# Ternary signs prepared in the offset stage, and the hats of tile columns loaded from ScalarE's queue

## Chip, cores, metric

One core of one Trainium2 chip. The metric is the time on the device of one execution, in microseconds (us). The four executions of the kernel before agree within 0.2% (7741.9 to 7756.0 us), those of the changed kernel within 0.5% (8181.8 to 8218.1). All executions that were timed in rounds ran in the fast state; runs of one look have no state of their own; the kernel before, run beside them, took 7741 to 7753 us (medians). The engines are PE (TensorE), DVE (VectorE), ACT (ScalarE), POOL (GpSimd) and SP (SyncE, which here only issues transfers, 5,333 in the kernel before).

## The reference, cut to what matters

```python
def _branch(x, w_off, w_def, lw, lb, pad, dil):          # dil = pad = 1, 9, 12
    off = _conv(x, w_off, pad, dil)                      # offsets, 18 channels
    y = _deform_dw(x, off, w_def, pad, dil)              # bilinear samples, 9 taps
    return gelu(_ln2d(y, lw, lb))
...
out = _ln2d(x1 + x2 + x3 + conv1x1(x), n1_w, n1_b)       # then an MLP and another _ln2d
...
def _L1_conv_ref(x, weight, bias, Wp, Wn):
    wq = _quantize(weight, Wp, Wn)                       # +Wp, 0 or -Wn by a threshold on max|w|
    return conv3x3(x, wq) + bias
...
x = x + _L0_conv_ref(_gn(x), ...)                        # x: (2, 256, 128, 128) float32
x = x + _L1_conv_ref(_gn(x), ...)
```

## The kernel before

It has three stages. The **offset stage** normalises `x`, computes the offsets of all branches and writes "hats" (the weights of bilinear interpolation along rows and along columns) to memory. The **sampling stage** treats 402 units: 2 batches x 67 tile rows x 3 branches. A unit loads three row hats `hy` and three column hats `hx`, DVE multiplies them to `A`, PE samples by multiplying the table's tiles `xs` with `A`, ACT copies each product to `ev`, DVE adds `ev` into `ring`. A tail (norms, MLP) is woven in. The **convolution stage** works with signs of the weights.

```python
def load_tiles(b, Rt):
    for T in range(NT):                                            # 14 tiles
        xt = pool.tile([P, C], F32, name="xs", tag="xs", bufs=20)
        ...
        nc.sync.dma_start(xt, src)

def load_hats(u):
    for ky in taps(u):                                             # up to three
        hy = pool.tile([P, RI, 3, W], F32, name="hy", tag="hy", bufs=3)
        hx = pool.tile([P, RI, 3, W], F32, name="hx", tag="hx", bufs=3)
        for h, first, dims in ((hy, ...), (hx, ...)):
            nc.sync.dma_start(h[...], ...)                         # both from SyncE

def sample(u, c):                                                  # two passes, c = 0 and 1
    ev = pool.tile([P, 9 * RI, NT * CI], F32, name="ev", tag="ev", bufs=2)
    for T in range(0, NT, 2):
        if T // 2 == NT // 4:
            tail.advance()
        pm = psum.tile([P, 2, 256], F32, name="pm", tag="pm", bufs=4)
        for j in range(2):
            pin(nc.tensor.matmul(pm[:, j, 0:n], lhsT=xts[...], rhs=A[...], ...))
        pin(nc.scalar.copy(ev[...], pm[...]))
    if c == KC - 1:
        prepare(u + 2)                     # build(u + 2), then load_hats(u + 3)
    accumulate(u, c, ev, kys)
...
# offset stage: statistics of each batch, through three buffers
xt = ap.tile([P, XT * NG], F32, name="xt", tag="xt", bufs=3)
nc.sync.dma_start(xt, ...)
nc.vector.bn_stats(...)
...
# convolution stage
signs = cp.tile([P, KC, 9, C], BF16, name="signs")
quantise(cp, signs)                        # loads the weights, threshold, 18 x 3 instructions
```

`pin` keeps an instruction at its place in its engine's order.

Of the kernel before, what the change touches and what calls it, by code (L numbers as in the profile page):

```python
# [67 lines left out]
def conv_preact_kernel(ctx: ExitStack, tc: tile.TileContext, t: dict, out: bass.AP):  # L68
# [19 lines left out]

    def load(name, shape, src):
        tl = const.tile(shape, F32, name=name)  # L90
        nc.sync.dma_start(tl, src)
        return tl

    gmask = load("gmask", [P, P], t["gmask"])
    convs = [
# [18 lines left out]

    def dram(name, shape):
        return [scratch.tile(shape, F32, name=f"{name}{b}", tag=f"{name}{b}") for b in range(NB)]
# [8 lines left out]
    yd = scratch.tile([3, C, HW], F32, name="yd")  # L125

# [33 lines left out]
    def phase_a(b, pool, psum, k):  # L160
# [160 lines left out]
        for g in range(NGRP):  # L321
            columns(g)
            while G < H // ZG and min(H - 1, G * ZG + ZG - 1 + max(DILS)) < (g + 1) * R:
                parts = offsets(G)
                for j in range(ZG // R):
                    make_hats(G * (ZG // R) + j, parts, j * R)
                G += 1

    with ExitStack() as actx:
# [18 lines left out]
        nc.sync.dma_start(k["wz"], t["wz"].rearrange("(k p) n -> p k n", p=P))  # L348
        nc.sync.dma_start(k["shift"], t["shift"])
        hatw = ap.tile([P, 2, NTAP * NH], F32, name="hatw32")  # L350
        nc.sync.dma_start(hatw, t["hatw"])
        nc.vector.tensor_copy(k["hatw"], hatw)
        pattern = ap.tile([P, NG], F32, name="pattern")
        nc.sync.dma_start(pattern[HALF : HALF + NPAT], t["pattern"])
        for pl in k["planes"]:
            nc.vector.tensor_copy(
                pl[HALF : HALF + NPAT, 1, :], pattern[HALF : HALF + NPAT]
            )
        for parts in k["parts"]:
            nc.vector.memset(parts, 0.0)  # L360
        XT = min(4, NGRP)
        for b in range(NB):
            stats = ap.tile([P, KC, NGRP, 6], F32, name=f"stats1_{b}", tag=f"stats1_{b}")
            for c in range(KC):
                for g0 in range(0, NGRP, XT):
# [7 lines left out]
                    for j in range(XT):  # L373
                        nc.vector.bn_stats(stats[:, c, g0 + j, :], xt[:, j * NG : (j + 1) * NG])
            mean, rstd = group_norm(stats, f"gn1_{b}", gps)
# [7 lines left out]
            phase_a(b, ap, psum, k)  # L383
# [8 lines left out]
    beyond = nc.values_load(flag[0:1, 0:1], min_val=0, max_val=1)  # L392

# [231 lines left out]
    def sample_near(pool, psum, k):  # L625
# [4 lines left out]
        xts, hbs, owners, begun = {}, {}, {}, set()  # L630
        done = {(b, br): 0 for b in range(NB) for br in BRS}
# [23 lines left out]
        def load_hats(u):  # L655
            b, Rt, br = units[u]
            for ky in taps(u):
# [6 lines left out]
                for h, first, dims in (  # L664
                    (hy, 0, [[0, TC], [pitch, TR]]),
                    (hx, TR, [[pitch, TC], [0, TR]]),
                ):
                    src = hq[first, y0]
                    nc.sync.dma_start(
                        h[:, i0:i1].rearrange("p i t w -> p (i t w)"),  # L670
                        bass.AP(src.tensor, src.offset, dims + [[1, (i1 - i0) * 3 * W]]),
                    )
                hbs[u, ky] = hy, hx

# [67 lines left out]
        def sample(u, c):  # L742
# [4 lines left out]
            if not kys:  # L747
                tail.advance()
# [7 lines left out]
            for T in range(0, NT, 2):  # L756
                if T // 2 == NT // 4:
                    tail.advance()
                pm = psum.tile([P, 2, 256], F32, name="pm", tag="pm", bufs=4)
# [31 lines left out]
        load_hats(0)  # L791
        prepare(0)
        prepare(1)
        for u, (b, Rt, br) in enumerate(units):
# [128 lines left out]
    def quantise(pool, signs=None):  # L923

        wq = pool.tile([P, KC, 9, C], F32, name="wq", tag="wq", bufs=1)
        nc.sync.dma_start(wq, t["l1w"].rearrange("(k p) t o -> p k t o", p=P))
        scale = []
        for name in ("wp", "wn"):
            s = pool.tile([P, 1], F32, name=name, tag=name, bufs=1)
            nc.sync.dma_start(s, t[name].partition_broadcast(P))  # L930
            scale.append(s)
        wp, wn = scale
        nc.vector.tensor_scalar(wn, wn, -1.0, None, ALU.mult)

        def col(name):
            return pool.tile([P, 1], F32, name=name, tag=name, bufs=1)

        own, m, mh, ml, pr, er, z, nc_ = (
            col(f"q_{i}") for i in ("own", "m", "mh", "ml", "pr", "er", "z", "nc")
        )  # L940
        nc.vector.tensor_reduce(
            own, wq.rearrange("p k t o -> p (k t o)"), AX.X, ALU.max, apply_absolute_value=True
        )
        nc.gpsimd.partition_all_reduce(m, own, P, bass.bass_isa.ReduceOp.max)  # L944



        def ts(dst, a, s1, op0, s2=None, op1=None):
            nc.vector.tensor_scalar(dst, a, s1, s2, op0, *(() if op1 is None else (op1,)))

        ts(mh, m, 4097.0, ALU.mult)
        nc.vector.tensor_tensor(ml, mh, m, ALU.subtract)
        nc.vector.tensor_tensor(mh, mh, ml, ALU.subtract)
        nc.vector.tensor_tensor(ml, m, mh, ALU.subtract)
        ts(pr, m, THR, ALU.mult)
        nc.vector.scalar_tensor_tensor(er, mh, THR_HI, pr, ALU.mult, ALU.subtract)
        nc.vector.scalar_tensor_tensor(er, mh, THR_LO, er, ALU.mult, ALU.add)
        nc.vector.scalar_tensor_tensor(er, ml, THR_HI, er, ALU.mult, ALU.add)
        nc.vector.scalar_tensor_tensor(er, ml, THR_LO, er, ALU.mult, ALU.add)
        nc.vector.scalar_tensor_tensor(er, m, THR_HALF_ULP, er, ALU.mult, ALU.add)  # L960

        ts(z, m, 0.0, ALU.is_equal)
        nc.vector.tensor_tensor(pr, pr, z, ALU.add)
        ts(nc_, er, -1.0, ALU.mult)
        for k in range(KC):
            for tap in range(9):
                w = wq[:, k, tap, :]
                up = pool.tile([P, C], F32, name="up", tag="up", bufs=1)
                ts(up, w, pr, ALU.subtract, er, ALU.is_ge)
                dn = pool.tile([P, C], F32, name="dn", tag="dn", bufs=1)  # L970
                ts(dn, w, pr, ALU.add, nc_, ALU.is_le)
                if signs is not None:
                    nc.vector.tensor_tensor(signs[:, k, tap, :], up, dn, ALU.subtract)  # L973
                    continue
                ts(up, up, wp, ALU.mult)
                nc.vector.scalar_tensor_tensor(w, dn, wn, up, ALU.mult, ALU.add)
        return wq

# [51 lines left out]
    def phase_c_signs(b, pool, psum, cring, signs, sums, wp, half):  # L1030
# [9 lines left out]
        JC = RC // 2  # L1040
        for g in range(H // RC):
# [4 lines left out]
            for k in range(KC):  # L1046
                nc.sync.dma_start(xl[:, k, rows, :], xv[:, k, lo:hi, :])
            xc = cring[g % len(cring)]
            for k in range(KC):
# [16 lines left out]
                left = D.rearrange("p i j w -> p (i j) w")  # L1066
                for i in range(2):
                    part = xc[:, i, k, :, 1 : 1 + W]
                    nc.scalar.copy(part, left)  # L1069
                    nc.vector.tensor_tensor(  # L1070
                        left if i == 0 else xc[:, 2, k, :, 1 : 1 + W], left, part, ALU.subtract
                    )
            for m in range(KC):
                pc = psum.tile([P, 4, 512], F32, name="pc", tag="pc", bufs=2)

                for bank, t in ((0, 0), (1, 3), (2, 1), (3, 2)):
# [3 lines left out]
                    for j, (k, kx, i) in enumerate(todo):  # L1080
                        w = (
                            signs[:, k, (t // 3 * 2) * 3 + kx] if t % 3 == 0
                            else sums[:, k, t - 1, kx]
# [30 lines left out]

    wpn = small.tile([P, 2], F32, name="wpn", tag="wpn", bufs=1)
    for i, name in enumerate(("wp", "wn")):
        nc.sync.dma_start(wpn[:, i : i + 1], t[name].partition_broadcast(P))
    eq = const.tile([P, 1], I32, name="eq")
    nc.vector.tensor_tensor(eq, wpn[:, 0:1], wpn[:, 1:2], ALU.is_equal)
    same = nc.values_load(eq[0:1, 0:1], min_val=0, max_val=1)  # L1120

    with tc.If(same > 0) as cmp:  # L1122
        with ExitStack() as cctx:
# [10 lines left out]
            signs = cp.tile([P, KC, 9, C], BF16, name="signs")  # L1134
            quantise(cp, signs)

            sums = cp.tile([P, KC, 2, 3, C], BF16, name="sums")
            for k in range(KC):
                nc.vector.tensor_tensor(
                    sums[:, k, 0], signs[:, k, 0:3], signs[:, k, 6:9], ALU.add  # L1140
                )
                nc.vector.tensor_tensor(
                    sums[:, k, 1], sums[:, k, 0], signs[:, k, 3:6], ALU.subtract
                )
                nc.vector.tensor_tensor(
                    sums[:, k, 0], sums[:, k, 0], signs[:, k, 3:6], ALU.add
                )
            half = cp.tile([P, 2], F32, name="half")
            for i in range(2):
                nc.vector.tensor_scalar(  # L1150
                    half[:, i : i + 1], wpn[:, 0:1], 0.5 - i, None, ALU.mult
                )
            for b in range(NB):
                phase_c_signs(b, cp, psum, cring, signs, sums, wpn[:, 0:1], half)
# [102 lines left out]
```

## Time and profile before

| | before |
|---|---|
| median of all its runs beside the changed kernel | 7751.5 us |
| offset stage, first `pz` product to first `pm` product | 880 us |
| sampling stage, first `pm` to the last store of `x1d` | 5,696 us |
| convolution stage, from there to the end | 1,094 us |

From the page of the kernel before: the busy time of the engines, then groups of instructions (line, engine, operation, output<-inputs, count | busy, mean ns of one | idle time before them and what ended it).

```profile
PE 7065.1 (91%) x37984; PEld 5377.1 (69%) x37984; DVE 6136.4 (79%) x12892; ACT 4818.2 (62%) x10138; POOL 708.7 (9%) x1292
...
L762 PE MATMUL pm<-A,xs 128*128 128x180 f32 (+2 forms) x22288 | 3609.6, 318 | 466.8 <-ACT ev L771 438.3
```

PE is the fullest engine, and nearly all its idle time in the sampling stage is ended by ACT having copied a product. The 62% of ACT look like plenty of room. That this number misleads is one lesson of this case.

### The profile page before, as it was taken

To read this page: it belongs to the slowest core of one execution; us is meant where nothing else is said; L and a number is where in the kernel's file an instruction comes from. 1 tells how busy PE (TensorE), PEld (TensorE's weight loads), DVE (VectorE), ACT (ScalarE), POOL (GpSimd) and SP (SyncE) were. 2 spreads that over 40 slices of the span, in tenths; PEclk is the share of its full clock that TensorE was granted. 3 is DMA by queue.
4 is the path that set the end of the run, shared out by engine and by line. 5 is a ranking of instruction groups with operands and counts; after the bars stand their busy time and mean duration, and the time that the engine had idled before them with its cause. 6 is when DMAs were issued, how large, how long until landed. Compare 5 with 4: busy or idle time off the path is not lost. (4 is left out here: it accounts for less than half of the span.)

```text
span 7751.0 us, 115301 instructions
## 1 busy us (share of the span) xinstructions
PE 7065.1 (91%) x37984; PEld 5377.1 (69%) x37984; DVE 6136.4 (79%) x12892; ACT 4818.2 (62%) x10138; POOL 708.7 (9%) x1292
## 2 busy tenths in 40 slices
PE   5999888999999999999988999999999998699999
PEld 3555587787877788777777778777887776244444
DVE  6666568888888888888678888888888885677676
ACT  1344366777777777777766777777777776333232
POOL 0000000111111111111101111111111111000000
PEclk9999889999999999999999999999999998799999
DMA  8776799999999999998699999999999994212121
GB/s 296 212 197 190 191 235 249 249 255 251 246 252 252 252 247 251 254 245 229 184 235 247 255 249 250 247 251 255 247 249 253 251 241 133 85 74 75 70 75 49
DMA packets 1011325, 1652.64 MB, mean 213 GB/s; under 512 B 120800, under 2 KB 573200, under 8 KB 1006360
## 3 DMA queue, kind: packets, MB, share of 16 engines
q1 hardware_dynamic: 993304, 1611.57, 77.7%
q10 hardware_dynamic: 17408, 33.56, 1.4%
q8 instruction: 304, 4.98, 0.3%
q14 instruction: 309, 2.53, 0.1%
HBM read 1376.69 MB, written 268.09 MB: 212 GB/s over the span
## 5 line engine op out<-in xcount | busy, mean ns | idle before, releaser
L762 PE MATMUL pm<-A,xs 128*128 128x180 f32 (+2 forms) x22288 | 3609.6, 318 | 466.8 <-ACT ev L771 438.3
L762 PEld LDWEIGHTS pm<-A,xs 128*128 128x128 f32 x22288 | 3407.1, 195 | 680.7 <-ACT ev L771 545.8
L740 DVE SCALAR_TENSOR_TENSOR ring<-ev,defw,ring 128x256 f32<-128x256 f32 (+3 forms) x6272 | 2774.5, 462 | 359.7 <-ACT ev L771 175.2
L771 ACT COPY ev<-pm 128x360 f32<-128x360 f32 (+2 forms) x5572 | 2235.8, 455 | 1131.6 <-DVE ring L740 462.9
L689 DVE TENSOR_TENSOR A<-hy,hx 128x768 f32<-128x768 f32 x1130 | 1022.3, 946 | 424.2 <-DMA hx<-hats 246.5
L487 ACT ACTIVATE T<-T,rs 128x256 f32<-128x256 f32 x1280 | 662.5, 593 | 3.3 <-POOL rs L483 3.2
L480 POOL TENSOR_SCALAR rs<-mv 128x4 f32<-128x4 f32 x320 | 120.7, 377 | 4981.0 <-DVE mv L478 2392.1
L1085 PE MATMUL pc<-cring,signs 128*128 128x512 bf16 x2304 | 521.9, 385 | 57.8 <-DVE signs L973 24.3
L1085 PE MATMUL pc<-cring,sums 128*128 128x512 bf16 x2304 | 510.3, 380 | 0.0
L446 PE MATMUL hp<-T,w 128*128 128x512 f32 x1024 | 492.7, 606 | 12.9 <-ACT T L565 12.9
L476 DVE BATCH_NORM_STATS2 st<-T 128x6 f32<-128x256 f32 x1280 | 446.8, 411 | 23.6 <-ACT T L468 23.6
L1085 PEld LDWEIGHTS <-signs 128*128 128x128 bf16 x2304 | 227.3, 99 | 341.8 <-issue 46.6
L203 PE MATMUL pz<-wz,xa 128*128 128x486 f32 x1024 | 456.7, 579 | 4.3 <-DVE zr L210 4.3
L446 PE MATMUL h<-hT,w 128*128 128x512 f32 x1024 | 460.1, 592 | 0.0
L1085 PEld LDWEIGHTS <-sums 128*128 128x128 bf16 x2304 | 225.4, 98 | 274.4
L515 ACT ACTIVATE T<-zc,bb,bw 128x512 f32<-128x512 f32 x384 | 278.7, 781 | 220.2 <-PE zc L499 219.7
L733 ACT ACTIVATE ring<-ev,defw 128x256 f32<-128x256 f32 (+1 forms) x788 | 392.2, 503 | 24.1
L499 PEld LDWEIGHTS zc<-ident,T 128*128 128x128 f32 x2560 | 325.9, 151 | 97.5 <-issue 61.5
L1093 ACT ACTIVATE o<-xl,l1b 128x1024 f32<-128x1024 f32 x64 | 73.5, 1149 | 505.7 <-DMA out_x<-o 408.3
L499 PE MATMUL zc<-ident,T 128*128 128x128 f32 x2560 | 368.7, 289 | 20.1 <-ACT T L487 13.9
L1069 ACT CAST cring<-D 128x2048 bf16<-128x2048 f32 x128 | 243.3, 1902 | 225.0 <-PE pc L1085 153.7
L482 POOL TENSOR_TENSOR rs<-rs,mhalf 128x4 f32<-128x4 f32 x320 | 368.3, 1151 | 0.0
(120 smaller groups left out, 5814.0 us busy)
## 6 DMA issues: line engine op xcount, KB each, us to landing
hy<-hats SPq DMA_DIRECT2D x1114, 384.0 KB, 6.5
hx<-hats SPq DMA_DIRECT2D x1114, 384.0 KB, 7.4
xs<-table SPq DMA_DIRECT2D x1876, 128.0 KB, 4.4
g12d<-T SPq DMA_DIRECT2D x128, 512.0 KB, 7.5
other<-g12d SPq DMA_DIRECT2D x128, 512.0 KB, 10.3
hats<-hb SPq DMA_DIRECT2D x192, 240.0 KB, 4.3
hats<-hb SPq DMA_DIRECT2D x192, 192.0 KB, 3.4
xl<-x1d SPq DMA_DIRECT2D x56, 640.0 KB, 3.9
```

Of the source, the lines that this page charges most:

```text
L203: nc.tensor.matmul(pz[:, 0:NZ], lhsT=xt[:, c, r, :], rhs=k["wz"][:, c, :], start=c == 0, stop=c == KC - 1,)
L446: nc.tensor.matmul(out, lhsT=w, rhs=v, start=i == 0, stop=i == n - 1)
L476: pin(nc.vector.bn_stats(st[:, j, :], Tv[:, j, :]))
L482: nc.gpsimd.tensor_tensor(rs[:, 0, :], rs[:, 0, :], mhalf[:, 0:NB4], ALU.pow)
L487: nc.scalar.activation(Tv[:, j, :], Tv[:, j, :], AF.Identity, scale=rs[:, 0, j : j + 1], bias=rs[:, 1, j : j + 1],)
L499: nc.tensor.transpose(zc[:, j * P : (j + 1) * P], Tv[:, j, c * P : (c + 1) * P], ident)
L689: nc.vector.tensor_tensor(dst, hy[:, i0:i1].rearrange("p i t w -> p t i w"), hx[:, i0:i1].rearrange("p i t w -> p t i w"), ALU.mult,)
L733: pin(nc.scalar.mul(dst, src, w))
L740: pin(nc.vector.scalar_tensor_tensor(dst, src, w, dst, ALU.mult, ALU.add))
L762: nc.tensor.matmul(pm[:, j, 0:n], lhsT=xts[b, Rt][T + j][:, c * P : (c + 1) * P], rhs=A[:, m0:m1, AO + (T + j) * CI : AO + (T + j + 1) * C ...
L771: nc.scalar.copy(ev[:, m0:m1, T * CI : (T + 2) * CI].rearrange("p m (t j) -> p t m j", j=CI), pm[:, :, 0:n].rearrange("p t (m j) -> p t m ...
L1085: nc.tensor.matmul(pc[:, bank, :], lhsT=w[:, m * P : (m + 1) * P], rhs=xc[:, i, k, t * JC : (t + 1) * JC, kx : kx + W], start=j == 0, stop ...
```

## The change

Three things were meant: let `x` go ahead of the constants at the start; take the signs out of the convolution's start by working them out amid the offset stage, where PE is the limit (busy 177.9 of 180 us); and let column hats no longer stand in SyncE's order behind tiles that wait for buffers. The core of the diff (cut; the loads of constants, and a finer split of the first convolution group, are left out):

```diff
+    def store_signs(pool):                       # a generator, one step per column group
+        w = pool.tile([P, 5, C], F32, name="wk", tag="xt", bufs=3)   # shares xt's buffers
+        ...
+            nc.sync.dma_start(signd[:, k], sg)
@@ offset stage
             columns(g)
+            next(beside, None)
@@ load_hats
-                    nc.sync.dma_start(
+                    args = (
                         h[:, i0:i1].rearrange("p i t w -> p (i t w)"),
                         bass.AP(src.tensor, src.offset, dims + [[1, (i1 - i0) * 3 * W]]),
                     )
+                    if h is hy:
+                        nc.sync.dma_start(*args)
+                    else:
+                        asked.append(args)
+        def load_columns():
+            while asked:
+                pin(nc.scalar.dma_start(*asked.popleft()))
@@ sample
                 if T // 2 == NT // 4:
                     tail.advance()
+                    load_columns()
@@ convolution stage
-            signs = cp.tile([P, KC, 9, C], BF16, name="signs")
-            quantise(cp, signs)
+            signs = cp.tile([P, KC, 15, C], BF16, name="signs")
...
+            if first:
+                nc.sync.dma_start(signs, signd)
```

## The prediction

> **What bounds the kernel now.** The program runs in three stages: offsets, deformable sampling with a tail of norms and MLP woven in, then the ternary convolution. I read the windows view first, with edges where the line groups change.
>
> ```profile
> core 0: us, PE busy (x) PEld busy (x) DVE busy (x) ACT busy (x) POOL busy (x), PEclk, DMA share, GB/s
> 250.00:430.00 180.00, 177.90 (x741) 100.41 (x741) 115.91 (x259) 75.03 (x140) 0.00 (x0) 1.00 0.75 211
> ...
> 1100.00:3600.00 2500.00, 2295.57 (x13233) 1984.65 (x13234) 2162.50 (x4827) 1850.80 (x4110) 311.78 (x555) 0.98 0.96 250
> ...
> 6713.00:6740.00 27.00, 20.73 (x72) 7.73 (x73) 23.72 (x45) 3.81 (x2) 0.00 (x0) 0.78 0.00 1
> 6740.00:6780.00 40.00, 40.00 (x186) 18.08 (x185) 27.45 (x32) 10.74 (x7) 0.00 (x0) 1.00 0.25 92
> ```
>
> The reader is to see that PE is busy nearly without a gap in the offset stage (177.9 of 180 us) and in the settled convolution (40 of 40), so there only PE work or the edges of a stage can change the time. In the sampling stage, some 5,700 of the 7,751 us, PE is busy 92% and DVE 86%: 204 us of PE idle in 2,500. The waits view of 1100 to 3600 us tells whose they are.
>
> ```profile
> PE pm L762 <- ACT ev L771: 199.9, 123, 6.1
> ...
> ACT ev L771 <- DVE ring L740: 219.5, 119, 7.0
> ...
> DVE A L689 <- DMA hx<-hats: 104.8, 69, 5.6
> ```
>
> It is one chain. PE waits for a PSUM bank that ACT has not copied; ACT waits for the `ev` buffer that DVE has not read; DVE, which has little slack, was held up at `A = hy*hx` because `hx` had not landed. The hats of tile columns are late in 69 of the 523 builds. Why are they late? The SyncE queue's own waits, and one case in the timeline:
>
> ```profile
> SPq L669 <- DVE A L689: 768.7, 216, 11.5
> SPq L643 <- PE pm L762: 394.5, 556, 4.8
> ```
>
> ```profile
> 2043.12 0.55 SPq L669 DMA_DIRECT2D hy<-hats  x1
> ...
> 2044.98 5.87 SPq L643 DMA_DIRECT2D xs<-table  x8
> ...
> 2050.90 0.59 SPq L669 DMA_DIRECT2D hx<-hats  x1
> ...
> 2052.18 0.59 SPq L669 DMA_DIRECT2D hx<-hats  x1
> ...
> 2058.63 0.96 DVE L689 TENSOR_TENSOR A<-hy,hx 128x768 f32<-128x768 f32 x1 [1.43 <-DMA hx<-hats]
> ```
>
> Between two hats loads of one unit SyncE issues eight `xs` tiles, each waiting for PE to free a buffer. The hats behind them start 7 us late, and the third build waits 1.43 us. I found this once per tile row (three units, 43 us) wherever I looked.
>
> [...] issuing one `hx` takes 0.59 us in the median (0.51 to 2.27). On ACT this stops later copies from being fed. [...] granted 0.50 up to 6685 us, 0.78 from 6713 to 6740.
>
> **The change, part by part.**
>
> *Start.* Small constants went ahead of `x` on SyncE. The DMA engines moved 62 and 38 GB/s from 12 to 15 and 15 to 18 us and 425 right after; the first `xt` issue is at 17.7 us and statistics end at 73.4. With `x` first, that issue moves to about 1.5 us. The same 3.1 MB of constants must still arrive before the first `pz`, and ScalarE's 2 MB of `xa` now compete, so I count not 16 but 10 us.
>
> *Signs in the offset stage.* Moved work on DVE: a maximum over 4608 elements, 4.95 us; 18 x (0.40 + 0.41 + 0.42) = 22 us; six sums of 0.55 = 3.3; scalars about 2. Sum 32 us, plus 4.7 MB of weight loads (read twice) and 2 MB of stores. PE bounds this stage and DVE has 35% free, but not for nothing: from 120 to 240 us, when batch 1's statistics (34 us of DVE) run beside it, PE was busy 109 of 120 us, against 119.7 of 120 from 280 to 400. So 11 us were lost for 34; the new steps are shorter and spread over 25 column groups: I take +6 us. They share the three `xt` buffers with batch 1's statistics, which then start later, but those ended at 238 us and are needed at 490.
>
> *Convolution stage.* The chain there is: weights land, maximum 6668.3 to 6673.2, maximum over partitions at 6676.6, signs from 6681.8 tap by tap between other DVE work. PE did 18 products from 6685 to 6695, stood 18 us waiting for signs, did 36 from 6713, waited 6 us more and is steady from 6735.7. By then it had done 18 + 36 + 15 = 69; a settled one takes 0.2165 us (110 us / 509 from 6740 to 6850 is 0.216), so 14.9 us of work: as if it had begun at 6720.7. After the change the signs are one 2 MB load, behind 1.2 MB of `xl`: at 370 GB/s, the rate in this stretch, about 9 us after 6660. The first products now need group norm (6667.3, unmoved), two normalisations (0.9 each), eight differences (0.6 each): 6674; then a quarter of the split, about 2.5 us: 6676.5. [...] So 6680.5: 40 us sooner, of which I leave 4 for DVE not having the second group ready. **-36 us.** The second batch's stall near 7230 us stays, as the finer split is only for the first group.
>
> *Sampling stage.* Removed: DVE's waits for `hx`. For each of the 119 waits of ACT for DVE I followed DVE's busy run back and added the DMA waits in it: at most 115 of the 219 us could go in 1100 to 3600, 103 of 209 in 3950 to 6350. PE's idle follows ACT's waits almost one to one, so the ceiling is about 218 us. I expect 60% of it, since `hy` still stands behind `xs`, and `hx` is now issued later than the moment its buffer falls free: **-130**. Added: three issues of 0.59 us a unit on ACT, amid a pass, 402 units: 1.8 us in 14.2 us of a unit, where ACT is 74% busy. The four PSUM buffers give PE about 2.5 us of slack, but in several passes PE wanted the fourth bank just when ACT freed it. And ACT must wait there until DVE has built the unit before: setting the end of the third build against ACT's fourth copy, it came 2.2 us too late in one of six passes I looked at, about in time in the rest. I take 0.17 us lost a unit: **+70**. Net **-60**.
>
> Sum: -10 + 6 - 36 - 60 = -100: 7754 to 7654.
>
> **Rivals.** (1) *ACT becomes the brake.* Its order is fixed, so a DMA issue that waits for DVE holds copies behind it, and PE stops with all banks full. For: ACT waits of up to 7 us on DVE already. Against: where ACT waits for DVE, DVE is the limit and does not need those copies yet. If each unit lost 0.6 us, +240 - 130 - 40 gives about 7825. (2) *The lateness is bandwidth, not order.* With DMA engines at 96%, splitting rings brings `hx` no sooner and pushes `hy` or `xs` back. For: `hx` takes 7.3 us to land in the median[...]. Against: the share falls to 0.55 and 0.43 in two-microsecond stretches at 2030 and 2042. Then sampling gains nothing and loses a little: about 7725 to 7760. (3) *All hats come in time:* -218, little ACT cost, -40 at the edges: about 7500 to 7540.
>
> **Range and chances.** The edges are fairly sure (-25 to -50). Sampling is the doubt: -170 to +40. So 7555 to 7750 holds it 8 times in 10. Over 2% faster means under 7599, a sampling gain of at least 115: 0.23. Over 2% slower means above 7909: 0.03. The rest, 0.74, is within 2%.
>
> **What would show it.** Step by step: the first `pz` near 70 us instead of 80; the page's offset stage no longer than before by more than 10 us; steady products within 20 us of the first `xl` instead of 74; in 1100 to 3600, DVE's wait for `hx` below 40 us and PE idle down from 204 to some 175; ACT's queue with 1,130 `hx` issues of about 0.6 us. I am wrong if DVE's wait moves to `hy`, if PE's wait for `ev` stays at 200 us while ACT waits less for DVE (rival 1), or if `hx` lands no sooner (rival 2).

## The result, and the profile after

The changed kernel takes 8201.6 us in the median (8181.8 to 8218.1, 4 runs) against 7751.5 us (7741.9 to 7756.0, 4 runs). The ratio is 1.058, 95% interval 1.055 to 1.061: **slower**, far outside the predicted range. Ratios here are the mean time of one kernel's fast runs over that of the other's of the same rounds, so not quite the ratio of the medians quoted. The outputs are correct.

By stage, in the profiled runs: to the first `pz` 80.4 -> 72.0 us, offset stage 880 -> 909, **sampling stage 5,696 -> 6,149**, convolution stage 1,094 -> 1,050. Everything bad and more than all the loss is in the sampling stage: +453 us. The page of the changed kernel, the lines that answer to those shown of before:

```profile
PE 7249.7 (89%) x37984; PEld 5486.5 (67%) x37984; DVE 6161.8 (75%) x12907; ACT 4783.0 (58%) x10150; POOL 663.2 (8%) x1292
...
L898 PE MATMUL pm<-A,xs 128*128 128x180 f32 (+2 forms) x22288 | 3779.4, 326 | 735.0 <-ACT ev L907 542.3
```

The same 22,288 recorded products have 268 us more idle time before them (735.0 - 466.8), and take 170 us more themselves (3779.4 - 3609.6): 438 of the 453. ACT, whose copies PE waits for, is *less* busy than before. The windows view says the same of 1100 to 3600 us, in the middle of the stage. The numbers are start:end, length, then the busy time of PE, PE's weight loads, DVE, ACT and POOL, each with its count, then PE's mean granted clock, the share of the DMA engines and GB/s:

```profile
250.00:430.00 180.00, 159.51 (x616) 86.58 (x615) 125.12 (x265) 61.10 (x115) 0.00 (x0) 0.92 0.81 236
1100.00:3600.00 2500.00, 2185.99 (x12083) 1873.48 (x12084) 1998.75 (x4428) 1688.09 (x3767) 260.55 (x500) 0.95 0.90 230
...
7148.00:7188.00 40.00, 40.00 (x178) 17.79 (x178) 39.96 (x50) 18.15 (x16) 0.00 (x0) 0.96 0.23 84
```

PE is 110 us less busy than before in the sampling window (2185.99 against 2295.57), with a granted clock of 0.95 against 0.98, and the DMA engines are less loaded, 0.90 against 0.96. No engine is at its limit. In the offset stage (first line) PE lost 18 of 180 us. The settled convolution (last line) is as before. The waits view of 1100 to 3600 (us in total, times, longest us):

```profile
PE pm L898 <- ACT ev L907: 238.3, 150, 8.7
DVE ring L874 <- ACT ev L907: 200.7, 99, 7.8
...
ACT ev L907 <- DVE ring L874: 151.3, 101, 4.8
...
ACT ev L907 <- DMA hy<-hats: 93.6, 16, 8.9
...
PE pm L898 <- DMA xs<-table: 72.3, 28, 4.8
...
DVE A L823 <- DMA hx<-hats: 32.3, 24, 3.2
```

What the change aimed at came true: DVE's wait for column hats fell from 104.8 to 32.3 us. But PE, and now DVE as well, wait for ACT's copies. And there is a line that makes no sense by the data: ACT's copy `ev <- pm` needs no `hy`, yet it stood 16 times until a transfer of `hy` had landed. One case in the timeline (start, length, engine, line, operation, count, and in brackets the idle time before):

```profile
2020.52 4.36 ACTq L807 DMA_DIRECT2D hx<-hats  x3
...
2020.52 2.63 SPq L799 DMA_DIRECT2D hy<-hats  x3
...
2024.91 1.55 ACT L907 COPY ev<-pm 128x360 f32<-128x360 f32 x4 [4.68 <-DVE st L600]
...
2025.43 3.97 PE L898 MATMUL pm<-A,xs 128*128 128x180 f32 x12 [3.43 <-ACT ev L907]
```

Three issues of 0.52 us each should be through in 1.6 us; here they take 4.36, and PE stood 3.43 us until ACT had copied a product. The third issue waited, by the semaphore events in the trace, for a completion semaphore last used by an `xs` tile issued at 2019.88, whose last update came at 2024.27. The same events, in the order of ACT's queue (start and end in us, semaphores by their number in the trace):

```
2020.52 2021.05 hx<-hats issued, signals 100
2021.09 2021.43 waits for 108 and 103
2021.46 2021.99 hx<-hats issued, signals 103
2024.30 2024.31 waits for 106
2024.35 2024.87 hx<-hats issued, signals 106
2024.91 2025.37 ev<-pm copied
```

The tile of 2019.88 signals 106 too. In this trace the 5,405 transfers that SyncE and ScalarE issue signal eight semaphores between them, 675 or 676 transfers each. Of these issues 5,099 come after a wait for the very semaphore that they signal, and in 5,372 of the 5,397 reuses the trace has 16 updates between one issue and the next on the same semaphore, the same count each time, which fits the earlier transfer having landed, whatever it carried and whoever had issued it. Of the 486 issues of ACT in 1100 to 3600 us, 333 took a semaphore last used by a transfer of SyncE. In the same window SyncE's tiles waited 43 times for column hats to land, 26.4 us in sum. SyncE issued nothing but transfers, so there only transfers came later; on ACT the copies behind the issues stood, 4.68 us in this case.

The semaphore events of the trace say how much of ACT's waiting this is, in 1100 to 3600 us. Between and just before its three issues ACT waits 1.42 us a unit. Waits of 0.86 us end with a landing, nearly always of the transfer that last used the semaphore the issue is about to take (0.53 us for tiles, 0.23 for row hats); waits of 0.44 us end with a product of DVE.

That a wait for another queue's transfer is what costs the time is tested below.

### The profile page after: what moved, and what is told of

It is laid out like the page before. It is cut to its first block, busy times and chain, and to the rows that moved or that the text cites. A ratio compares the mean times of both kernels' runs of the same rounds, so it can differ in the third digit from the quotient of the medians.

```text
span 8180.0 us, 116312 instructions
## 1 busy us (share of the span) xinstructions
PE 7249.7 (89%) x37984; PEld 5486.5 (67%) x37984; DVE 6161.8 (75%) x12907; ACT 4783.0 (58%) x10150; POOL 663.2 (8%) x1292
## 5 line engine op out<-in xcount | busy, mean ns | idle before, releaser
L898 PE MATMUL pm<-A,xs 128*128 128x180 f32 (+2 forms) x22288 | 3779.4, 326 | 735.0 <-ACT ev L907 542.3
L898 PEld LDWEIGHTS pm<-A,xs 128*128 128x128 f32 x22288 | 3512.3, 200 | 1010.9 <-ACT ev L907 759.7
L907 ACT COPY ev<-pm 128x360 f32<-128x360 f32 (+2 forms) x5572 | 2191.3, 453 | 1551.1 <-PE pm L898 529.1
L1184 PE MATMUL pc<-cring,signs 128*128 128x512 bf16 x4608 | 1005.6, 381 | 20.0 <-ACT cring L1131 13.3
L1184 PEld LDWEIGHTS <-signs 128*128 128x128 bf16 x4608 | 452.0, 98 | 573.0 <-issue 27.5
L592 ACT COPY T<-tp 128x512 f32<-128x512 f32 x640 | 340.0, 585 | 28.0 <-PE tp L590 27.7
L1131 ACT CAST cring<-D 128x2048 bf16<-128x2048 f32 (+1 forms) x140 | 245.0, 1755 | 183.3 <-PE pc L1184 124.7
L427 ACT ACTIVATE hb<-ph 96x512 f32<-96x512 f32 (+1 forms) x384 | 211.4, 592 | 187.8 <-PE ph L419 177.1
```

The lines of the kernel that those rows point to most:

```text
L898: nc.tensor.matmul(pm[:, j, 0:n], lhsT=xts[b, Rt][T + j][:, c * P : (c + 1) * P], rhs=A[:, m0:m1, AO + (T + j) * CI : AO + (T + j + 1) * C ...
L907: nc.scalar.copy(ev[:, m0:m1, T * CI : (T + 2) * CI].rearrange("p m (t j) -> p t m j", j=CI), pm[:, :, 0:n].rearrange("p t (m j) -> p t m ...
L1184: nc.tensor.matmul(pc[:, bank, :], lhsT=w[:, m * P : (m + 1) * P], rhs=xc[:, i, k, t * JC : (t + 1) * JC, kx : kx + W], start=j == 0, stop ...
```

## The experiments

**Theories.** T1, semaphores: ACT is held by issues that wait for the landing of other queues' transfers. T2, products (my rival 1): it is held because a column hat's buffer is free only after DVE's multiplication. T3, bare time: three issues cost ACT 1.7 us a unit, and that is enough. T4, transfers: with two queues the tiles and row hats come late, ACT only shows it.

The stages of all runs, from the profiled execution of each (us):

| run | offset | sampling | convolution | time |
|---|---|---|---|---|
| before | 880 | 5,696 | 1,094 | 7751 |
| changed | 909 | 6,149 | 1,050 | 8202 |
| e1_undo_columns | 909 | 5,696 | 1,052 | 7716 |
| e2_columns_alone | 893 | 6,145 | 1,094 | 8229 |
| e3_columns_second_pass | 906 | 6,215 | 1,052 | 8246 |
| e4_columns_pool | 916 | 5,728 | 1,050 | 7762 |
| d1_tiny_loads | 907 | 5,891 | 1,050 | 7915 |
| d2_copies | 906 | 5,887 | 1,052 | 7912 |
| d3_wait_for_product | 918 | 5,750 | 1,050 | 7785 |
| d4_one_of_three | 896 | 5,824 | 1,050 | 7838 |
| d6_wide_tiny | 912 | 5,966 | 1,050 | 7996 |
| e6_tiles_pool | 904 | 5,825 | 1,051 | 7846 |
| e7_undo_tiles_pool | 904 | 6,045 | 1,050 | 8072 |
| g1_signs_in_batch_1 | 892 | 5,682 | 1,052 | 7703 |
| d7_six_copies | 899 | 6,528 | 1,052 | 8550 |
| h2_rows_pool | 910 | 6,151 | 1,050 | 8178 |

Runs e1 to e4 were timed in 3 rounds, g1 in 5; the others are one look each, good for some 20 to 50 us (e1's four runs span 20 us, e2's 47).

How long ACT is held, in 1100 to 3600 us: from the start of the first to the end of the last issue of a unit (most units have three), mean over the units, and of it the issues' own time; for copies, their busy time. The expectations of d6, e6 and d7 below quote an earlier count (2.0 and 3.1 us held, 1.3 and 1.4 us of waiting), which had joined the issues of different units here and there; the table tells the units apart by the program's own order.

| run | held, us a unit | own time | rest: waiting between them |
|---|---|---|---|
| changed | 2.72 (443.1 / 163) | 1.68 | 1.04 |
| e3_columns_second_pass | 3.00 (486.5 / 162) | 1.69 | 1.31 |
| d1_tiny_loads | 1.87 (319.2 / 171) | 0.73 | 1.14 |
| d2_copies | 1.58 (267.7 / 169.7) | 1.58 | 0 |
| d6_wide_tiny | 2.22 (375.5 / 169) | 1.24 | 0.98 |
| e6_tiles_pool | 2.21 (384.9 / 174) | 1.71 | 0.51 |
| d7_six_copies | 3.15 (480.6 / 152.5) | 3.15 | 0 |
| h2_rows_pool | 2.47 (404.7 / 164) | 1.62 | 0.85 |

Before the first issue of a unit ACT waits another 0.38 us in the changed kernel and 0.27 in h2; in e3, d1, d6 and e6 about 0.05.

### Which part of the change it is

```diff
 # e1_undo_columns, on the changed kernel
-                    if h is hy:
-                        nc.sync.dma_start(*args)
-                    else:
-                        asked.append(args)
+                    nc.sync.dma_start(*args)
```

> The changed kernel with the column hats issued by SyncE again, the rest of the change kept. If the whole loss lies in ScalarE's issues (all theories of the sampling stage), the sampling stage returns to the 5,696 us of the kernel before, and what is left is start -8, offset stage +29, convolution stage -44: 7,728 us, ratio 0.995 to 1.000. If the new order of DVE's work, or the colder clock, comes from the signs, the stage stays above 5,850 us and the time above 7,880 us.

Measured: 7715.8 us (7706.4 to 7726.1), ratio 0.9944 (0.9925 to 0.9964). The sampling stage is back at 5,696 us to the microsecond.

```diff
 # e2_columns_alone, on the kernel before: asked, load_columns() and its calls as in the change
+                    if h is hy:
+                        nc.sync.dma_start(*args)
+                    else:
+                        asked.append(args)
```

> The kernel before with only the column hats moved to ScalarE's queue. If the loss is that part alone: the sampling stage 6,150 us as in the changed kernel (5,696 + 453) and the time 8,204 us, ratio 1.055 to 1.062. If the signs and the hats act on each other, the ratio is under 1.04.

Measured: 8228.6 us, ratio 1.0625 (1.0594 to 1.0656). The column hats on ScalarE are the whole loss; the rest of the change is a small gain. That the two parts act on each other does not show beyond the noise.

### Not the wait for DVE's products

```diff
 # e3_columns_second_pass, on the changed kernel
-                    load_columns()
+                    if c == KC - 1:
+                        load_columns()
```

> The changed kernel with the ScalarE issues put in the middle of the unit's second pass, some 7 us later, when DVE has long made the three products that free the buffers. If the wait for DVE's products (my rival 1) is what holds ScalarE, most of the 453 us goes: 7,750 to 7,850 us, less if DVE then waits for column hats that start only some 4 us before their product. If the wait is for a shared DMA-completion semaphore whose earlier transfer has not landed, whatever it carries, or the plain issue time of 3 x 0.53 us, ScalarE is held as before and it stays at 8,050 to 8,250 us.

Measured: 8246.5 us, ratio 1.0633 (1.0612 to 1.0653). Seven microseconds later the products are done: of 483 issues in the window one began within 0.12 us of a DVE event that it waited for, against 176 of 486 in the changed kernel. Yet ACT is held about as long: 3.05 us a unit with the wait before the first issue, against 3.10. The run is not quite clean, as the hats now start late for their use:

```profile
DVE A L823 <- DMA hx<-hats: 297.1, 243, 4.9
```

So d3 tests the product wait by itself, without any transfer:

```diff
 # d3_wait_for_product, on e1
-                pin(nc.scalar.dma_start(*asked.popleft()))
+                v, ky = asked.popleft()
+                ... # o: first column of what build(v - 1, ky) writes
+                pin(nc.scalar.copy(spare, Aw[:, o : o + 1]))     # one column, 0.19 us
```

> The same with three ScalarE copies of one column (some 0.2 us each) in the place of the loads, each reading what one of DVE's three newest products has written: ScalarE waits for the same products as the column hats' buffers did, without any DMA. If rival 1 (the wait for DVE) is the cause: over 7,950 us. If it is the semaphores or the issue time: under 7,800 us.

Measured: 7784.9 us, 69 us over e1. The three copies take 0.57 us a unit, and at the price that d2 will show for ACT's time (197 us for 1.58 us) they account for 71 us alone. The waits were real, and by that price nearly free:

```profile
ACT spare L812 <- DVE A L828: 118.3, 137, 4.0
```

ACT stood 118 of 2,500 us for the products, and the run lost little by it. T2 falls as the main cause. A small part for it stays possible: the price of ACT's time is not linear (d7 below), so the copies alone may cost less than 71 us, and this is one look.

### What ACT's bare time costs

```diff
 # d2_copies, on e1
-                pin(nc.scalar.dma_start(*asked.popleft()))
+                asked.popleft()
+                pin(nc.scalar.copy(spare, spare))                # 128x400 floats
```

> The same with three ScalarE copies of 128x400 floats (some 0.5 us each, so 1.5 us a unit against 1.7 us for three issues) in the place of the loads. If time taken from ScalarE in the middle of the first pass is the whole cause: 8,000 to 8,200 us. If the wait for shared semaphores is the cause, ScalarE's bare time costs only what I predicted for it, +70 us: 7,750 to 7,820 us.

Measured: 7912.4 us, +197 over e1, between the two expectations. So 1.58 us of ACT a unit cost 0.49 us a unit (197 / 402), nearly three times what I had put down for the same length (0.17), but under half of the loss. T3 is true, and 1.68 us of issues alone do not suffice.

```diff
 # d1_tiny_loads, on e1
+                tiny = pool.tile([1, 64], F32, name="tiny", tag="tiny", bufs=3)
+                pin(nc.scalar.dma_start(tiny, t["gmask"][0:1, 0:64]))
 # d6_wide_tiny, on e1
+                tiny = pool.tile([P, 8], F32, name="tiny", tag="tiny", bufs=3)
+                pin(nc.scalar.dma_start(tiny, t["gmask"][:, 0:8]))
```

> The kernel with the column hats back on SyncE (7,716 us), plus three loads of 256 bytes a unit issued by ScalarE where the changed kernel issues its column hats; nothing reads them, they wait for no DVE product and load the DMA engines with nothing. If ScalarE is held by shared completion semaphores or by the issue time itself, the loss of the changed kernel comes back without the hats: 8,050 to 8,250 us. If it was the wait for DVE's products, or the row and column hats coming from two queues at once, it stays under 7,790 us.

Measured: 7914.6 us, +199, above the bound of T2 and T4 (7,790) and below that of T1 and T3 (8,050). The issue of a tiny load took only 0.22 us, so by d2's price (an estimate) its 0.73 us a unit are worth some 90; the other 110 then come from waiting 1.14 us a unit. These loads need no product and move next to nothing; still ACT waits for landings of SyncE's transfers, by the semaphore events for row hats (0.39 us a unit), tiles (0.35) and stores of `x1d` (0.27):

```profile
ACT ev L908 <- DMA xs<-table: 91.1, 31, 5.4
...
ACT ev L908 <- DMA tiny<-in_gmask: 48.8, 43, 4.2
```

In e1 such waits are absent from the same window. This is T1 in isolation: for a load of 256 bytes ScalarE waits for a transfer of SyncE.

> As the three tiny loads of a unit, which cost 199 us, but over all 128 partitions with 32 bytes each: the issue then takes ScalarE what a column hat's issue takes (0.53 us against the 0.22 us of the tiny ones), and almost nothing is moved. The tiny loads held ScalarE 2.0 us a unit (0.7 of issue, 1.3 of waiting for semaphores of earlier transfers), the column hats 3.1. If issue and semaphores are the whole loss: 1.6 + 1.3 = 2.9 us a unit and 8,080 to 8,180 us. If the hats' own transfers, late tiles or the product waits are a good part of it: under 8,020 us.

Measured: 7996.5 us, +281, a miss: below both lines. My assumption about the issue was wrong, for 128 rows of 32 bytes it took 0.35 us in the median, not 0.53, and the waits were 0.98 us. Held time and loss both lie between those of d1 and of the changed kernel, so the run fits T1 with T3 but leaves room for another 200 us.

```diff
 # d4_one_of_three, on the changed kernel
-                    if h is hy:
+                    if h is hy or ky:
```

> The changed kernel with only the middle one of the three column hats of a unit on ScalarE, the others on SyncE. If each issue costs ScalarE alike, a third of the 486 us comes back: 7,850 to 7,910 us. If ScalarE has slack for the first one (it stood idle 649 of 2,500 us), under 7,790 us. If one late semaphore a unit is enough to do the harm, over 7,960 us.

Measured: 7838.5 us, between the first two expectations: one issue a unit costs 123 us over e1, three cost 486. There is some slack for the first, but the first is not free.

### The tiles issued by GpSimd

That GpSimd's transfers do not share SyncE's and ScalarE's semaphores was my assumption. What the run shows is how often ScalarE still waits for a landing.

```diff
 # e6_tiles_pool, on the changed kernel, in load_tiles
-                nc.sync.dma_start(xt, src)
+                nc.gpsimd.dma_start(xt, src)
```

> The changed kernel with the table's tiles issued by GpSimd[...]. They are the most frequent transfers among those that share semaphores with the column hats, and wait longest. If shared semaphores are the larger part of the loss, ScalarE's waits between its three issues (1.4 us a unit) shrink under 0.5 us and the time falls to that of the three plain copies: 7,860 to 7,960 us. If they are not, it stays at 8,100 us or more. If GpSimd's small work for the normalisations comes late behind the tiles, new waits for its results show up.

Measured: 7846.4 us: 355 of the 486 us are back, with the column hats still on ScalarE and the same issue time. The waits between the issues fell from 1.04 to 0.51 us, at the edge of the 0.5 expected, and those that ended with a landing from 0.63 to 0.08. Of 514 issues in the window 16 had a landing as the last thing they waited for, against 129 of 486 in the changed kernel; what is left is mostly products (0.33 us a unit, as before). In the timeline the three issues now follow one another:

```profile
2034.76 0.59 ACTq L807 DMA_DIRECT2D hx<-hats  x1
...
2035.44 0.56 ACTq L807 DMA_DIRECT2D hx<-hats  x1
...
2036.76 0.52 ACTq L807 DMA_DIRECT2D hx<-hats  x1
...
2037.32 1.55 ACT L907 COPY ev<-pm 128x360 f32<-128x360 f32 x4
```

This happened though PE waited for tiles as long as in the changed kernel over the whole run (181.3 us against 187.5) and ACT for GpSimd's results 113.6 instead of 4.0. So late tiles are not what cost the time. But e6 changes more than these waits: it also takes the tiles out of SyncE's order, and without ScalarE's loads that alone costs 356 us (e7 below). So 355 us is not a clean price of the shared semaphores.

> The changed kernel with the row hats, not the tiles, issued by GpSimd[...]. ScalarE's column hats still share semaphores with the tiles. If it is the tiles (most of the transfers, waiting for their buffers) on whose landing ScalarE waits, ScalarE's waits between its issues stay over 1 us a unit and the time over 8,050 us. If the two kinds of hats hold each other up, the waits fall under 0.6 us a unit and the time to 7,850 to 7,950 us.

```diff
 # h2_rows_pool, on the changed kernel, in load_hats
                     if h is hy:
-                        nc.sync.dma_start(*args)
+                        nc.gpsimd.dma_start(*args)
```

Measured: 8177.8 us, no better than the changed kernel, as expected for the tiles. The waits between the issues, 0.85 us a unit, lie between the two expectations: with the wait before the first issue counted in, the 0.23 us for row hats is gone, but ScalarE now waits 0.65 us for tiles instead of 0.53. So the tiles are the larger part, and they alone keep the loss up.

> As the run with three copies a unit on ScalarE (+197 us for 1.6 us a unit), with six: 3.2 us a unit, as long as the column hats' issues hold ScalarE in the changed kernel (3.1 us from the start of the first to the end of the third). If the length of the hold on ScalarE is the whole cause, whatever it is made of: 8,110 (twice 197) to 8,260 us. If a good part comes from SyncE's tiles and row hats being held back by ScalarE's transfers: under 8,050 us.

```diff
 # d7_six_copies: d2 with two copies for each hat, six a unit
```

Measured: 8549.8 us, +834 over e1, beyond both expectations. Holding ACT 3.15 us a unit, about as long as the changed kernel does (2.72 us, 3.10 with the wait before the first issue), is more than enough for the whole loss, without one shared semaphore and with tiles in time (PE's waits for them: 2.1 us in the window). The price is not linear. The first 1.58 us a unit cost 197 us, the second, equal, 637: 1.58 us a unit, its full length. The windows view of d2 and of d7 shows where the limit lies:

```profile
1100.00:3600.00 2500.00, 2250.15 (x12744) 1908.09 (x12742) 2091.09 (x4657) 2006.64 (x4472) 287.69 (x526) 0.98 0.93 241
```

```profile
1100.00:3600.00 2500.00, 2086.14 (x11310) 1789.93 (x11311) 1877.37 (x4136) 2035.01 (x4435) 252.47 (x464) 0.94 0.84 216
```

ACT is busy 80% in the one and 81% in the other: in this chain of PE, ACT and DVE twice the copies did not fill it further, and each further microsecond lengthened the unit. The 74% of the kernel before (1850.80 of 2500) were close to that. In the changed kernel ACT has 1688 us of busy time and 443 us of holding, 85% together (an upper estimate, as ACT also computed meanwhile: one activation ran from 1725.31 to 1725.91 us, over issues from 1725.02 to 1725.54 and 1725.66 to 1726.19). Why its loss is smaller than d7's for a hold of like length no run separates; that overlap, and column hats in time, would both work that way.

### Can the hats come in time at all?

```diff
 # e4_columns_pool, on the changed kernel
-                pin(nc.scalar.dma_start(*asked.popleft()))
+                nc.gpsimd.dma_start(*asked.popleft())
```

> The changed kernel with the column hats issued from GpSimd's queue, which has nothing else to do in this stage. The transfers, their bytes and buffers stay. If it is the hold on ScalarE (by semaphores, products or issue time), the loss goes and DVE's waits for column hats (247 us before) stay small: 7,600 to 7,740 us. If it is the load of the DMA engines or the row hats now coming out of order, it stays above 8,000 us.

Measured: 7761.9 us, ratio 1.0002 (0.9984 to 1.002), outside both expectations. The hold on ACT is gone, and so is nearly all waiting for column hats: over the whole run 13.5 us, against 246.5 before. But the sampling stage is 32 us *longer* than with all hats on SyncE. The wait went elsewhere:

```profile
DVE A L823 <- DMA hy<-hats: 185.5, 127, 10.6
...
PE pm L898 <- DMA xs<-table: 177.6, 93, 4.7
```

In the kernel before neither is among the hundred largest waits of the whole run. The DMA engines are 96% busy in the window, as before, so this fits my rival 2: what one queue gains the other loses. No run frees the DMA engines to test that alone.

```diff
 # e7_undo_tiles_pool: e1 with the tiles on GpSimd, as in e6
```

> The kernel with the column hats back on SyncE (7,716 us), with the tiles on GpSimd's queue. If the column hats are late because they stand behind tiles that wait for their buffers in SyncE's order, which is what the change wanted to mend, DVE's waits for them (105 us in the window 1100 to 3600) nearly vanish: 7,600 to 7,680 us. If they are late because the DMA engines are full (busy share 0.95), 7,700 to 7,740 us. If GpSimd then comes late with its own work, over 7,760 us.

Measured: 8071.9 us, the third of the expected cases, and worse than I had thought. DVE's waits for column hats halved (54.5 us in the window), but GpSimd, standing in front of tiles, is late with its small work for the norms, and DVE's products wait for PE:

```profile
DVE A L820 <- PE pm L895: 156.4, 56, 4.9
...
ACT T L611 <- POOL rs L607: 128.2, 28, 9.5
```

Why e6, with the same tiles on GpSimd and more for ACT to do, is 226 us faster than e7 I did not find out.

### The offset stage

In the changed kernel the second batch's statistics ran from 193 to 378 us instead of 105 to 238, since signs and statistics share the `xt` buffers. One case, from its timeline:

```profile
225.06 1.46 SPq L475 DMA_DIRECT2D xt<-in_x  x1
...
225.64 0.37 ACTq L296 DMA_DIRECT2D xa<-in_x  x1
...
236.37 0.55 DVE L173 TENSOR_SCALAR xa<-xa,gn_mean,gn_rstd 128x512 f32<-128x512 f32 x1 [6.71 <-DMA xa<-in_x]
...
238.24 0.29 PE L407 MATMUL pp<-ident_b,parts 128*128 128x128 bf16 x1 [6.83 <-DVE parts L397]
```

The statistics' load goes out just ahead of the column load, DVE stands 6.71 us for the latter, and PE as long for what DVE has behind it in its order. PE had seven such gaps before `pp`, 1.7 to 6.8 us, 28 us in sum; the kernel before had three, 1.6 to 6.2 us, 9.5 us in sum.

```diff
 # g1_signs_in_batch_1, on e1
-            phase_a(b, ap, psum, k, beside)
+            phase_a(b, ap, psum, k, beside if b else iter(()))
```

> The kernel with the column hats back on SyncE, with the signs worked out beside the second batch of the offset stage alone, so that the buffers they share with the second batch's statistics are free for these as early as before the change. If the loss of some 22 to 29 us in the offset stage comes from the statistics' loads landing among the column loads of the first batch: the offset stage falls from 909 to about 885 us and the time to 7,685 to 7,705 us, ratio 0.991 to 0.994. If it comes from the signs' own work and traffic, the stage stays near 909 us and the time at 7,716 us.

Measured: 7703.1 us (7691.7 to 7714.0, 6 runs), ratio 0.994 (0.9921 to 0.9959). The time is as expected; the offset stage fell to 892 us, not quite to 885, and the second batch's statistics ran from 100 to 245 us, as early as before the change. But the stage scatters: 896 to 918 over the thirteen runs with the changed order, 880 and 893 in the two with the old one. And e1's interval, taken in other rounds, overlaps g1's. That g1 beats e1 is therefore open; that both beat the kernel before, by some 0.6%, is shown (under 2%, so the verdict on both is "same").

## Why the prediction was wrong, step by step

- **Start** (-10): right, -8.4 us in the profiled pair; the first `pz` comes at 64 to 74 us in the other runs with the changed order, and at 83 in e2 with the old one.
- **Signs in the offset stage** (+6): the sign was right, the size not: +29 us in the profiled pair, +21 between the means of the thirteen runs with the changed order (907) and the two with the old one (887). The term that was mis-sized is the sentence that the statistics "then start later, but those ended at 238 us and are needed at 490". Later was harmless for who needs them, and harmful for whose loads they met. That this is all of it was only argued.
- **Convolution stage** (-36): right in size, -44, and not quite in its path. In the timeline of the changed kernel

```profile
7132.74 0.82 SPq L1142 DMA_DIRECT2D xl<-x1d  x2
...
7133.68 0.35 SPq L1145 DMA_DIRECT2D signs<-signd  x1
...
7143.24 0.58 PE L1184 MATMUL pc<-cring,signs 128*128 128x512 bf16 x1 [4.18 <-DMA signs<-signd]
...
7148.00 2.29 PE L1184 MATMUL pc<-cring,signs 128*128 128x512 bf16 x5 [1.09 <-DVE cring L1132]
```

  the first product waits for the signs' load, where the prediction had the split by DVE and ACT come last; the split was done sooner than it reckoned. Steady work begins 15.3 us after the first `xl`; predicted within 20. The 4 us from 6676.5 to 6680.5 in its reckoning were an estimate; the clock granted from 7132 to 7148 us was 0.50.
- **Sampling, removed** (-130): failed. DVE's waits for column hats did fall as foretold (104.8 to 32.3 us, foretold under 40), but in e4, without a burden on ACT, this brought nothing: the lateness moved to row hats and tiles. (The ceiling of 218 us was also the sum of two windows, 4,900 of the stage's 5,700 us.) That was my rival 2, which I put aside because of two short stretches with idle DMA engines.
- **Sampling, added** (+70): this is the step that failed, as put: "I take 0.17 us lost a unit". It counted three issues of 0.59 us on an engine that is busy 74%; the 2.5 us of slack answer to four buffers of two products, 318 ns each. Two things stood in its place. First, bare time on ACT was worth nearly three times as much (d2: 197 us). Second, the step had no term for the semaphores: ACT waited 0.86 us a unit for SyncE's transfers to land. With the tiles issued by GpSimd (e6), 355 us come back; the remaining 131 are the issues, with whatever the move of the tiles and hats in time bring to set against them. d7 shows that such a hold accounts for the loss without any late transfer.
- **Rival 1**, "a DMA issue that waits for DVE holds copies behind it", had the right victim and the wrong cause: ACT became the brake (in 1100 to 3600 us PE's wait for `ev` rose from 199.9 to 238.3 us while ACT's wait for `ring` fell from 219.5 to 151.3, the sign it had named), but waiting for DVE costs little (d3). It was also too mild, with 0.6 us a unit; 453 us / 402 is 1.13.
- Open: the split of the 170 us by which PE's products themselves got slower. In the window the granted clock was 0.94 or 0.95 in the five runs with the least busy PE (d7, e3, changed, e2, h2) against 0.98 in the kernel before, in d7 without any transfer moved. PE was busy 2086 us in d7, 2164 in e3, 2186 in the changed kernel and 2208 in h2, 2296 in the kernel before; e7 had 0.95 at 2243 us, d6 0.97 at 2234. In these runs the lower clock goes with the idling, roughly; no run separates the two.

## What to carry to other kernels

Here a unit's transfers issued from ScalarE cost it 1.68 us of issue time and 1.42 us of waiting, 0.86 of it for landings, nearly always of the transfer that last used the semaphore. An issue took it 0.53 us in the median for 128 rows of 3 KB, 0.35 for 128 rows of 32 bytes, 0.22 for one row of 256 bytes. Read the program's waits of each issue before moving it, and try it on an engine that has no copies behind it (GpSimd in e4: 7762 us against 8202). A busy share of 74% was no slack here, where three engines hand each buffer on: test it by adding a few plain copies, an experiment of a few lines. Moving a late transfer forward with the DMA engines 96% busy only changed what was late (e4: DVE's waits for column hats 13.5 us instead of 246.5, but 185.5 for row hats, and 177.6 of PE for tiles).
